# PSUM's eight banks divided among the engines that empty them, in a graph kernel's first layer

## The chip, the cores and the metric

The kernel runs on one core of one Trainium2 chip. A core has several engines with instruction streams of their own: TensorE (PE in the profile; its weight loads are PEld), VectorE (DVE), ScalarE (ACT), GpSimd (POOL) and SyncE (SP), which here issues transfers. Products and transposes of TensorE land in PSUM, which has eight banks; a bank holds 512 float32 values for each of 128 partitions. The metric is the device time of one execution in microseconds (us); lower is better.

## The reference

The input is 16 graphs of 1024 nodes with 128 features each, a dense symmetric-pattern adjacency with random positive weights (about 6% of the entries, and the diagonal), and a mask of ones. Two residual layers follow each other:

```
# layer 0
h = relu(layernorm(x))
for W, b in three layers:
    h  = h @ W + b
    nh = h / max(norm(h), 1e-12)
    ew = adj * (nh @ nh.T)            # per graph, 1024 x 1024
    h  = ew @ h                       # relu, but for the last
x = x + h
# layer 1
h = relu(layernorm(x))
keep = dilate(adj > 0)                # row by row, each row's removals change later rows
adj_d = adj * keep
three SAGE layers on adj_d with batch norm, then one linear map
x = x + that
```

The dilation depends on the adjacency alone, not on layer 0, so the kernel does it beside layer 0.

## The kernel before

**Layer 0.** The function `layer0()` is a generator. It walks over 48 stages: the graphs in pairs, each pair through the three convolutions, the two graphs of a pair taking turns. The list is `order`; of a stage `now`, `then` is the next, `after` the one behind it, and `ended` a graph that has just had its last convolution. A stage has eight steps s, one for each row q of 128-wide blocks, in the order SEQ = (0, 7, 1, 6, 2, 5, 3, 4). `ew` is as symmetric in its cosine part as `nh @ nh.T` is, so only the blocks on and above the diagonal are multiplied out. In a step:

- `products(s)`: TensorE multiplies the row's blocks of `nh @ nh.T` into PSUM tiles pg, of up to four blocks (L324). VectorE multiplies them with the adjacency, into ew in SBUF: the diagonal block at L333, the others at L336, which writes the row's blocks twice, with the weights of both triangles.
- `sums`, three steps behind (LAG): products of ew and the scaled features into po, which holds two banks (L364).
- `turn`: one step behind, the lower triangle's blocks are transposed on TensorE (gt, L353) and brought back to ew by ScalarE (L354).
- `sums_back`: products of the turned blocks into po (L378). After the last row ScalarE takes po up as hTo (L387).
- `adjT_tile` for the adjacency of a graph to come: transposes into pt_a (L240), taken up by ScalarE (L241), and stored for layer 1 by POOL (L242).
- `features` for the next stage at steps 4 and 5: products into pw (L273), taken up by VectorE as hN (L277 or L283). `turned` at step 6: transposes into pt_n, taken up by ScalarE as nhT (both L165 and L166, in `transposed`). `scaled`: squares on ScalarE (L299), the root (L157), and the scaling on POOL (L301).
- At the change from a pair to the next: `norm` and `enter` for the graphs that come (layer norm; transposes into pt_h, taken up by ScalarE); for the graphs that have ended `fetch` (the input is loaded again) at step 1, `residual` at step 3 (eight transposes into two tiles px, L398; VectorE adds the input, L401; POOL stores x2, L404) and `next_layer` at step 5 (layer norm for layer 1, stored by POOL, L410).

**The dilation.** The generator `dilation()` loads rows of the adjacency (an, L545), makes patterns on ScalarE (L547, L548), multiplies with what earlier rows kept (kl, L551; VectorE, L554), transposes small 16-bit tiles (pdt, pT; taken up by ScalarE, L571 and L580), iterates with counts in a tiny tile pc (L632, L633; VectorE), transposes pe (L681, ScalarE L682), and then runs for each row a scan of 1024 elements on VectorE (L699), an absolute value on ScalarE (L708) and a compare (L719), stored by POOL (L720).

**The order.** The main loop takes a unit of the dilation, and then as many units of layer 0 as the weights that both yield allow (COLS, TURN and SPREAD set the pace). This gives program order. The Tile framework then orders each engine's stream when the program is built, with program order as priority, and puts in the semaphores; a tile of a pool with n buffers waits until the tile n places before it under its tag is released. An engine runs its stream strictly in order. Behind layer 0 stand a branch (L768) that redoes the dilation exactly if the fast one was off (not taken for this input), the last graph's residual, and layer 1.

**PSUM.** Four pools hold the banks: ps_sm two for mt, pt_a, pt_h, pw, pt_n, px, pdt, pT, pc, pe and pf, whoever empties them; ps_g two for pg; ps_o one tile of two banks for po; ps_t two for gt. In SBUF, x2, h and h0 share two buffers under the tag tt, the loaded inputs two under xb, and the transposed features two under hT.

Of the kernel before, what the change touches and what calls it, by code (L numbers as in the profile page):

```python
# [8 lines left out]
F32 = mybir.dt.float32  # L9
F16 = mybir.dt.float16  # L10
# [3 lines left out]
PSUM = bass.MemoryType.PSUM  # L14
DRAM = bass.MemoryType.DRAM

P = 128
# [20 lines left out]
COLS, TURN = 0.215, 0.109  # L38
# [8 lines left out]
def tile_adj_preln_d2(  # L47
# [40 lines left out]
    nc = tc.nc  # L88
    B, N, D = x.shape
    NCH = N // P  # L90
    NB = B * NCH
    HALF = min(512, N)
    NHALF = N // HALF
    CPH = HALF // P
    GT = 4
# [16 lines left out]
    x2_d = [dram.tile([N, D], F32, tag=f"x2{b}", name=f"x2{b}") for b in range(B)]  # L112
# [47 lines left out]
    def transposed(psum_pool, dst, src, nm, func=AF.Copy, halves=range(NHALF)):  # L160

        for h in halves:
            pt = psum_pool.tile([P, CPH, P], F32, tag="sm", name=f"pt_{nm}_{h}")
            for c in range(CPH):
                nc.tensor.transpose(pt[:, c, :], src[:, h * CPH + c, :], ident)  # L165
            nc.scalar.activation(dst[:, h * CPH : (h + 1) * CPH, :], pt, func)  # L166


    with ExitStack() as actx:
        pool1 = actx.enter_context(tc.tile_pool(name="a1", bufs=1))  # L170
        pool2 = actx.enter_context(tc.tile_pool(name="a2", bufs=2))
        ps_sm = actx.enter_context(tc.tile_pool(name="a_sm", bufs=2, space=PSUM))
        ps_g = actx.enter_context(tc.tile_pool(name="a_g", bufs=2, space=PSUM))
        ps_o = actx.enter_context(tc.tile_pool(name="a_o", bufs=1, space=PSUM))
        ps_t = actx.enter_context(tc.tile_pool(name="a_t", bufs=2, space=PSUM))

        w0 = pool1.tile([P, 3, P], F32, name="w0")
        b0 = pool1.tile([P, 3, P], F32, name="b0")
# [23 lines left out]
        nc.scalar.dma_start(mi, nodemask.rearrange("b (c p) -> (b c) p", p=P))  # L202
        mfl = pool2.tile([P, NCH, P], F32, tag="tt", name="mfl")[:NB, 0, :]
        nc.vector.tensor_copy(mfl, mi)
        mt = ps_sm.tile([P, NB], F32, tag="sm", name="mt")
        nc.tensor.transpose(mt, mfl, ident[:NB, :NB])
        mf_flat = mf.rearrange("p b c -> p (b c)")
        nc.vector.tensor_copy(mf_flat, mt)
# [20 lines left out]
        def adjT_tile(b, q):  # L229

            place, nat, row = adj_place(b, q), Nat.pop((b, q)), NCH - q
            if row > 1:
                nc.sync.dma_start(
                    place[:, row:, :].rearrange("p c q -> p (c q)"), adj[b][q * P : (q + 1) * P, (q + 1) * P :]
                )
            for c in range(0, row, CPH):
                n = min(CPH, row - c)
                pt = ps_sm.tile([P, CPH, P], F32, tag="sm", name=f"pt_a{b}_{q}_{c}")
                for i in range(n):
                    nc.tensor.transpose(pt[:, i, :], nat[:, c + i, :], ident)  # L240
                nc.scalar.activation(place[:, c : c + n, :], pt[:, :n, :], AF.Copy)  # L241
            nc.gpsimd.dma_start(adjT_d[b][q][:, q * P :], place[:, :row, :].rearrange("p c q -> p (c q)"))  # L242

        class Batch:
# [15 lines left out]
            def enter(self, h):  # L260
                if h == 0:
                    self.hT = pool2.tile([P, NCH, P], F32, tag="hT", name=f"hT_{self.b}")
                transposed(ps_sm, self.hT, self.h, f"h{self.b}", halves=(h,))

            def features(self, h):

                nm, l, rn = f"{self.b}_{self.l}", self.l, self.rn
                if h == 0:
                    self.hN = pool1.tile([P, NCH, D], F32, tag="hN", bufs=1, name=f"hN_{nm}")
                hc = slice(h * CPH, (h + 1) * CPH)  # L270
                pw = ps_sm.tile([P, CPH, P], F32, tag="sm", name=f"pw_{nm}_{h}")
                for c in range(CPH):
                    nc.tensor.matmul(  # L273
                        pw[:, c, :], lhsT=self.hT[:, h * CPH + c, :], rhs=w0[:, l, :], start=True, stop=True
                    )
                if rn is None:
                    nc.vector.tensor_tensor(  # L277
                        self.hN[:, hc, :], pw, b0[:, l : l + 1, :].to_broadcast([P, CPH, P]), ALU.add
                    )
                else:  # L280
                    for c in range(CPH):
                        n = h * CPH + c
                        nc.vector.scalar_tensor_tensor(  # L283
                            self.hN[:, n, :], pw[:, c, :], rn[:, n : n + 1], b0[:, l, :], ALU.mult, ALU.add
                        )

            def turned(self):

                nhT = pool1.tile([P, NCH, P], F32, tag="nhT", bufs=2, name=f"nhT_{self.b}_{self.l}")
                transposed(ps_sm, nhT, self.hN, f"n{self.b}_{self.l}")  # L290
                self.next_nhT = nhT.rearrange("p c q -> p (c q)")

            def scaled(self):
# [50 lines left out]
            def turn(self, s, ew):  # L344

                q = SEQ[s]
                row = NCH - q
                for c in range(1, row, CPH):
                    n = min(CPH, row - c)
                    pt = ps_t.tile([P, CPH, P], F32, tag="gt", name=f"gt_{self.b}_{self.l}_{q}_{c}")  # L350
                    at = row + c - 1
                    for i in range(n):
                        nc.tensor.transpose(pt[:, i, :], ew[:, at + i, :], ident)  # L353
                    nc.scalar.activation(ew[:, at : at + n, :], pt[:, :n, :], AF.Copy)  # L354
# [34 lines left out]
                    )  # L389
                    self.l += 1  # L390

            def residual(self):
                b = self.b
                self.x2 = x2 = pool2.tile([P, NCH, D], F32, tag="tt", name=f"x2_{b}")
                for h in range(NHALF):
                    pt = ps_sm.tile([P, CPH, P], F32, tag="sm", name=f"px_{b}_{h}")
                    for c in range(CPH):
                        nc.tensor.transpose(pt[:, c, :], self.hT[:, h * CPH + c, :], ident)  # L398
                    for c in range(CPH):
                        n = h * CPH + c  # L400
                        nc.vector.scalar_tensor_tensor(  # L401
                            x2[:, n, :], pt[:, c, :], self.rn[:, n : n + 1], self.xb[:, n, :], ALU.mult, ALU.add
                        )
                nc.gpsimd.dma_start(x2_d[b].rearrange("(c p) d -> p c d", p=P), x2)  # L404

            def next_layer(self):
                b = self.b
# [11 lines left out]
        def layer0():  # L419
# [26 lines left out]
            for i, now in enumerate(order + [None]):  # L446
# [5 lines left out]
                for s in range(NCH if now else LAG):  # L452
                    q = SEQ[s]
# [24 lines left out]
                    if ended:  # L478
                        if s == 1:
                            ended.fetch()  # L480
                        if s == 3:
                            ended.residual()
                            yield NCH * TURN
                        if s == 5:
                            ended.next_layer()
                    if s == 5 and after and first(i + 2):
                        after.fetch()
# [39 lines left out]
        def dilate(k, half, exact):  # L527
# [14 lines left out]
            for i in range(BH):  # L542
# [21 lines left out]
                if i % GT == GT - 1:  # L564
                    four = range(i - GT + 1, i + 1)
                    bs_ = slice(i - GT + 1, i + 1)
                    pdt = ps_sm.tile([P, GT, P], F16, tag="sm", name=f"pdt{nk}_{i}")
                    for n, ii in enumerate(four):
                        nc.tensor.transpose(pdt[:, n, :], pattern(ii)[:, diag], ident16)
                    dT = pool2.tile([P, GT, P], F16, tag="dT", bufs=1, name=f"dT{nk}_{i}")  # L570
                    nc.scalar.activation(dT, pdt, AF.Copy)  # L571
                    nc.vector.tensor_scalar(rbias[:, bs_], rest[:, bs_], 2.0, -2.0, ALU.mult, ALU.add)
                    yield 0.1
                    pT = ps_sm.tile([P, GT, P], F32, tag="sm", name=f"pT{nk}_{i}")
                    for n, ii in enumerate(four):
                        nc.tensor.matmul(pT[:, n, :], lhsT=dT[:, n, :], rhs=upto, start=True, stop=False)
                        nc.tensor.matmul(pT[:, n, :], lhsT=pattern(ii)[:, diag], rhs=off, start=False, stop=False)
                        nc.tensor.matmul(pT[:, n, :], lhsT=ident16, rhs=after, start=False, stop=True)
                    for n, ii in enumerate(four):
                        nc.scalar.activation(T[:, ii, :], pT[:, n, :], AF.Identity, bias=rbias[:, ii : ii + 1])  # L580
                    yield 0.1
# [24 lines left out]
            def removals(x, nm):  # L606
# [13 lines left out]
                else:  # L620
# [4 lines left out]
                        nc.vector.tensor_tensor(ev, ev, x, ALU.is_gt)  # L625
                        nc.vector.scalar_tensor_tensor(par, x, 1.0, ev, ALU.is_gt, ALU.mult)
                    nc.vector.tensor_tensor(E, T, mid.unsqueeze(2).to_broadcast([P, BH, P]), ALU.is_equal)
                pc = ps_sm.tile([P, BH], F32, tag="sm", name=f"pc_{nm}")
                for i in range(BH):
                    c = pc[:, i : i + 1]  # L630
                    if ends:
# [44 lines left out]
            if ends:  # L676
                nc.vector.tensor_tensor(Z, Z, par.unsqueeze(2).to_broadcast([P, BH, P]), ALU.mult)
                nc.vector.tensor_tensor(E, E, Z, ALU.add)
            pe_ = ps_sm.tile([P, BH, P], F16, tag="sm", name=f"pe{nk}")
            for i in range(BH):  # L680
                nc.tensor.transpose(pe_[:, i, :], E[:, i, :], ident16)  # L681
            nc.scalar.activation(E, pe_, AF.Copy)  # L682
# [62 lines left out]
            while at * total < done * SPREAD * total0 and step0():  # L745
                pass

        pf = ps_sm.tile([1, B // 2], F32, tag="sm", name="pf")
        nc.tensor.matmul(pf, lhsT=ones_col, rhs=astray, start=True, stop=True)
        off_f = pool1.tile([1, 1], F32, name="off_f")  # L750
        nc.vector.tensor_reduce(off_f, pf, mybir.AxisListType.X, ALU.add)
# [374 lines left out]
```

## Time and profile before

| | us |
|---|---|
| runs shown (3): median | 2925.94 |
| lowest, highest | 2923.68, 2931.75 |
| the profiled execution | 2932.24 |
| its span, first to last instruction | 2930.4 |
| TensorE busy | 2673.3 (91%) |
| VectorE busy | 1955.9 (67%) |
| ScalarE busy | 1420.2 (48%) |
| GpSimd busy | 452.9 (15%) |
| granted TensorE clock, mean | 0.976 |

The last eviction of a turned block (L354) ends the first layer's main part at about 1723 us; layer 1 takes the rest. An engine's busy time is the time in which it worked on an instruction. A line of the view of waits names the engine, its tile and line, who released it, and then the microseconds in all, how often, and the longest. A line of the view of windows gives for each engine the busy time and the instructions in a stretch of the span. "L324" is line 324 of the kernel before.

### The profile page before, as it was taken

The numbers are of one execution on the slowest core, as the hardware profiler recorded it, in microseconds if no ns is written. First come the engines' busy times: TensorE is split into PE (matmuls) and PEld (weight loads), VectorE is DVE, ScalarE is ACT, GpSimd is POOL, SyncE is SP. The second block draws the span as 40 slices with busy tenths as digits, with TensorE's granted clock in tenths as the row PEclk, the third lists the DMA queues.
The fourth block names the chain that finished last, engine by engine and source line by source line (L and its number), as shares of the span: only waits on it lengthen the run. The fifth ranks groups of instructions, "written<-read, shape, count | busy, mean of one in ns | idle before, by whom it ended". The sixth has DMA issues, their size and how long they took to land.

```text
span 2930.4 us, 51972 instructions
## 1 busy us (share of the span) xinstructions
PE 2673.3 (91%) x18803; PEld 2205.6 (75%) x18803; DVE 1955.9 (67%) x4945; ACT 1420.2 (48%) x4069; POOL 452.9 (15%) x604
## 2 busy tenths in 40 slices
PE   5898998998989989998998979999989999899996
PEld 3666666666666666766666758989979999899996
DVE  2777778877977878788778446777772233455555
ACT  5766667557546546455455323333333333333333
POOL 2111112012011112121112002222220010010010
PEclk9999999999999999999999989999999999999998
DMA  8437258247347456386162039999995666576763
GB/s 268 145 115 219 89 168 247 77 139 229 92 130 219 105 169 188 95 248 176 39 206 105 1 114 403 405 406 404 405 372 173 208 210 202 177 243 222 240 217 115
DMA packets 383017, 585.21 MB, mean 200 GB/s; under 512 B 85201, under 2 KB 267345, under 8 KB 382753
## 3 DMA queue, kind: packets, MB, share of 16 engines
q1 hardware_dynamic: 343280, 425.28, 45.9%
q0 software_dynamic: 38464, 156.07, 14.4%
q8 instruction: 151, 2.47, 0.3%
q14 instruction: 114, 0.93, 0.1%
q10 hardware_dynamic: 1008, 0.46, 0.1%
HBM read 403.44 MB, written 163.58 MB: 193 GB/s over the span
## 4 chain that ended last, share of the span: by engine, by line
PE 56%; DVE 18%; DMA 13%; issue 6%; ACT 4%; POOL 1%; SPq 1%; POOLq 0%; DVEq 0%; another core or an unknown queue 0%; ACTq 0%
PE agg L831 20%; PE po L364 7%; PE pg L324 6%; DVE rank L699 5%; PE pw L803 5%; PE po L378 5%; DVE ew L336 4%; DMA aT<-in_adj_dram 3%; PE gt L353 3%; PE pp L1016 2%; DMA kl<-keep 2%; PE pw L273 2%; DMA an<-in_adj_dram 2%; DMA aT<-adjT 1%; DMA kb<-keep 1%
## 5 line engine op out<-in xcount | busy, mean ns | idle before, releaser
L831 PE MATMUL agg<-hw,aT 128*128 128x128 f32 (+1 forms) x6144 | 742.9, 277 | 8.8 <-DVE aT L941 7.5
L831 PEld LDWEIGHTS agg<-hw,aT 128*128 128x128 f32 x6144 | 712.1, 192 | 14.7 <-DVE aT L941 10.1
L324 PE MATMUL pg<-nhT 128*128 128x512 f32 (+3 forms) x1152 | 457.4, 500 | 71.9 <-DVE ew L336 63.0
L364 PE MATMUL po<-ew,hS 128*128 128x512 f32 (+3 forms) x1152 | 455.3, 499 | 13.8 <-ACT hTo L387 9.9
L336 DVE TENSOR_TENSOR ew<-pg,adjA 128x768 f32<-128x768 f32 (+3 forms) x528 | 425.1, 827 | 4.6 <-DVEq L768 2.7
L378 PE MATMUL po<-ew,hS 128*128 128x128 f32 x2688 | 366.9, 277 | 0.0
L378 PEld LDWEIGHTS po<-ew,hS 128*128 128x128 f32 x2688 | 339.3, 193 | 36.6 <-issue 36.3
L354 ACT ACTIVATE ew<-gt 128x512 f32<-128x512 f32 (+1 forms) x480 | 208.9, 465 | 243.2 <-PE gt L353 240.2
L324 PEld LDWEIGHTS pg<-nhT 128*128 128x128 f32 x1152 | 188.7, 193 | 171.6 <-issue 120.9
L699 DVE TENSOR_TENSOR_SCAN rank<-patt 128x1024 f16<-128x1024 f16 x128 | 294.0, 2307 | 0.9
L364 PEld LDWEIGHTS po<-ew,hS 128*128 128x128 f32 x1152 | 195.8, 194 | 105.6 <-issue 72.9
L353 PEld LDWEIGHTS gt<-ident,ew 128*128 128x128 f32 x1344 | 167.8, 143 | 97.3 <-issue 68.5
L333 DVE TENSOR_TENSOR ew<-pg,adjA 128x128 f32<-128x128 f32 x384 | 108.1, 282 | 196.3 <-PE pg L324 150.9
L353 PE MATMUL gt<-ident,ew 128*128 128x128 f32 x1344 | 212.1, 277 | 4.1 <-ACT ew L354 2.7
L881 POOL TENSOR_TENSOR o<-o,rn 128x512 f32<-128x512 f32 x96 | 107.6, 1121 | 650.4 <-DVE rn L880 646.0
L803 PE MATMUL pw<-wrx,hT 128*128 128x256 f32 x768 | 181.1, 391 | 10.2 <-ACT hT L1006 9.7
L805 DVE TENSOR_TENSOR own<-pw,bs 128x256 f32<-128x256 f32 x192 | 81.4, 424 | 148.0 <-ACT hw L804 148.0
L803 PEld LDWEIGHTS pw<-wrx,hT 128*128 128x128 f32 x768 | 146.3, 196 | 32.7 <-ACT hT L1006 10.5
L959 ACT ACTIVATE aT<-pta 128x512 f32<-128x512 f32 (+3 forms) x160 | 71.2, 466 | 205.0 <-PE pta L958 178.0
L860 DVE SCALAR_TENSOR_TENSOR o<-agg,invdeg,own 128x128 f32<-128x128 f32 x384 | 109.7, 344 | 87.0 <-PE agg L831 78.3
L876 ACT ACTIVATE own<-o 128x128 f32<-128x128 f32 x384 | 114.6, 301 | 103.3 <-DVE o L860 103.2
L301 POOL TENSOR_TENSOR hS<-hN,rn 128x1024 f32<-128x1024 f32 x48 | 94.6, 1970 | 409.2 <-DVE rn L157 300.4
(161 smaller groups left out, 3962.2 us busy)
## 6 DMA issues: line engine op xcount, KB each, us to landing
an<-in_adj_dram SPq DMA_DIRECT2D x128, 512.0 KB, 4.6
keep<-kp POOLq DMA_DIRECT2D x128, 256.0 KB, 3.6
kb<-keep SPq DMA_DIRECT2D x128, 256.0 KB, 5.4
aT<-adT SPq DMA_DIRECT2D x32, 960.0 KB, 5.4
aT<-adT SPq DMA_DIRECT2D x32, 832.0 KB, 5.5
aT<-adT SPq DMA_DIRECT2D x32, 704.0 KB, 4.6
aT<-adT SPq DMA_DIRECT2D x32, 576.0 KB, 3.4
xb<-in_x_dram SPq DMA_DIRECT2D x31, 512.0 KB, 5.1
```

The source lines that it names most:

```text
L324: nc.tensor.matmul(pg[:, :n, :].rearrange("p c q -> p (c q)"), lhsT=self.nhT[:, q * P : (q + 1) * P], rhs=self.nhT[:, (q + c) * P : (q + c ...
L333: nc.vector.tensor_tensor(ew[:, 0, :], pg[:, 0, :], place[:, 0, :], ALU.mult)
L336: nc.vector.tensor_tensor(both[0][:, :, off, :], pg[:, own:n, :].unsqueeze(1).to_broadcast([P, 2, n - own, P]), both[1][:, :, off, :], ALU ...
L353: nc.tensor.transpose(pt[:, i, :], ew[:, at + i, :], ident)
L354: nc.scalar.activation(ew[:, at : at + n, :], pt[:, :n, :], AF.Copy)
L364: nc.tensor.matmul(self.po[:, c * P : (c + n) * P], lhsT=self.hS[:, q, :], rhs=ew[:, c - q : c - q + n, :].rearrange("p c q -> p (c q)"), ...
L378: nc.tensor.matmul(self.po[:, q * P : (q + 1) * P], lhsT=self.hS[:, q + n, :], rhs=ew[:, NCH - 1 - q + n, :], start=False, stop=closes and ...
L699: nc.vector.tensor_tensor_scan(rank, pt[:, 1 : N + 1], pt[:, 2:], 0.0, ALU.add, ALU.add)
L803: nc.tensor.matmul(pw[:, i, :], lhsT=hT[:, 2 * h + i, :], rhs=wrx[:, l, :], start=True, stop=True)
L831: nc.tensor.matmul(self.place(c), lhsT=aT[:, blk, :], rhs=self.hw[:, source, :], start=source == 0 and c % self.ga == 0, stop=ends(c, source),
L860: nc.vector.scalar_tensor_tensor(self.o[:, c, :], self.place(c)[:, :P], invdeg[:, b, c : c + 1], self.own[:, c, :], ALU.mult, ALU.add,)
L876: nc.scalar.activation(self.own[:, n, :], self.o[:, n, :], AF.Square, accum_out=ss[:, c : c + 1])
```

## The change

The banks are divided by the engine that empties them. ps_v has one bank, for the tiles that VectorE takes up (mt, pw, px, pc, pf). ps_s has two, for those of ScalarE (pt_a, pt_h, pt_n, gt, pdt, pT, pe). ps_g has three instead of two, for pg. ps_o stays. The residual of a graph is made in two halves, the first at step 3 and the second, with the store of x2, at step 6; the layer norm behind it (`next_layer`) moves from step 5 to step 7. The weights yielded stay the same in sum. For the last graph both halves follow each other, as before.

```diff
-        ps_sm = actx.enter_context(tc.tile_pool(name="a_sm", bufs=2, space=PSUM))
-        ps_g = actx.enter_context(tc.tile_pool(name="a_g", bufs=2, space=PSUM))
+
+        ps_v = actx.enter_context(tc.tile_pool(name="a_v", bufs=1, space=PSUM))
+        ps_s = actx.enter_context(tc.tile_pool(name="a_s", bufs=2, space=PSUM))
+        ps_g = actx.enter_context(tc.tile_pool(name="a_g", bufs=3, space=PSUM))
         ps_o = actx.enter_context(tc.tile_pool(name="a_o", bufs=1, space=PSUM))
-        ps_t = actx.enter_context(tc.tile_pool(name="a_t", bufs=2, space=PSUM))
...
-                pt = ps_sm.tile([P, CPH, P], F32, tag="sm", name=f"pt_a{b}_{q}_{c}")
+                pt = ps_s.tile([P, CPH, P], F32, tag="sm", name=f"pt_a{b}_{q}_{c}")
...
-                transposed(ps_sm, self.hT, self.h, f"h{self.b}", halves=(h,))
+                transposed(ps_s, self.hT, self.h, f"h{self.b}", halves=(h,))
...
-                pw = ps_sm.tile([P, CPH, P], F32, tag="sm", name=f"pw_{nm}_{h}")
+                pw = ps_v.tile([P, CPH, P], F32, tag="sm", name=f"pw_{nm}_{h}")
...
-                transposed(ps_sm, nhT, self.hN, f"n{self.b}_{self.l}")
+                transposed(ps_s, nhT, self.hN, f"n{self.b}_{self.l}")
...
-                    pt = ps_t.tile([P, CPH, P], F32, tag="gt", name=f"gt_{self.b}_{self.l}_{q}_{c}")
+                    pt = ps_s.tile([P, CPH, P], F32, tag="sm", name=f"gt_{self.b}_{self.l}_{q}_{c}")
...
-            def residual(self):
+            def residual(self, halves=range(NHALF)):
                 b = self.b
-                self.x2 = x2 = pool2.tile([P, NCH, D], F32, tag="tt", name=f"x2_{b}")
-                for h in range(NHALF):
-                    pt = ps_sm.tile([P, CPH, P], F32, tag="sm", name=f"px_{b}_{h}")
+                if 0 in halves:
+                    self.x2 = pool2.tile([P, NCH, D], F32, tag="tt", name=f"x2_{b}")
+                x2 = self.x2
+                for h in halves:
+                    pt = ps_v.tile([P, CPH, P], F32, tag="sm", name=f"px_{b}_{h}")
...
-                nc.gpsimd.dma_start(x2_d[b].rearrange("(c p) d -> p c d", p=P), x2)
+                if 1 in halves:
+                    nc.gpsimd.dma_start(x2_d[b].rearrange("(c p) d -> p c d", p=P), x2)
...
-                        if s == 3:
-                            ended.residual()
-                            yield NCH * TURN
-                        if s == 5:
+                        if s == 3 or s == 6:
+                            ended.residual((s // 6,))
+                            yield CPH * TURN
+                        if s == 7:
                             ended.next_layer()
...
-                    pdt = ps_sm.tile([P, GT, P], F16, tag="sm", name=f"pdt{nk}_{i}")
+                    pdt = ps_s.tile([P, GT, P], F16, tag="sm", name=f"pdt{nk}_{i}")
...
-                    pT = ps_sm.tile([P, GT, P], F32, tag="sm", name=f"pT{nk}_{i}")
+                    pT = ps_s.tile([P, GT, P], F32, tag="sm", name=f"pT{nk}_{i}")
...
-                pc = ps_sm.tile([P, BH], F32, tag="sm", name=f"pc_{nm}")
+                pc = ps_v.tile([P, BH], F32, tag="sm", name=f"pc_{nm}")
...
-            pe_ = ps_sm.tile([P, BH, P], F16, tag="sm", name=f"pe{nk}")
+            pe_ = ps_s.tile([P, BH, P], F16, tag="sm", name=f"pe{nk}")
```

More of the change, by code (lines that the diff above doesn't have):

```diff
@@ L204, in tile_adj_preln_d2 @@
         nc.vector.tensor_copy(mfl, mi)
-        mt = ps_sm.tile([P, NB], F32, tag="sm", name="mt")
+        mt = ps_v.tile([P, NB], F32, tag="sm", name="mt")
         nc.tensor.transpose(mt, mfl, ident[:NB, :NB])
@@ L746, in tile_adj_preln_d2 @@
                 pass
-        pf = ps_sm.tile([1, B // 2], F32, tag="sm", name="pf")
+        pf = ps_v.tile([1, B // 2], F32, tag="sm", name="pf")
         nc.tensor.matmul(pf, lhsT=ones_col, rhs=astray, start=True, stop=True)
```

## Prediction

> **What bounds the kernel now.** I read the page's table of engines first, then a table by stage, then who TensorE, ScalarE and VectorE wait for in the stage that the change touches. Windows: the stretch, busy us of PE, PEld, DVE, ACT and POOL (instructions), granted TensorE clock, DMA share, GB/s.
>
> ```profile
> PE 2673.3 (91%) x18803; PEld 2205.6 (75%) x18803; DVE 1955.9 (67%) x4945; ACT 1420.2 (48%) x4069; POOL 452.9 (15%) x604
> ...
> 60.00:1600.00 1540.00, 1396.62 (x8734) 1016.25 (x8733) 1218.52 (x2853) 915.69 (x2430) 242.94 (x314) 0.98 0.53 154
> 1600.00:1710.00 110.00, 109.54 (x622) 79.76 (x620) 50.56 (x121) 36.81 (x114) 8.78 (x7) 1.00 0.02 6
> ...
> 870.00:880.00 10.00, 5.95 (x39) 4.59 (x38) 8.66 (x18) 5.34 (x13) 1.98 (x3) 0.98 1.13 287
> 880.00:890.00 10.00, 10.00 (x61) 7.92 (x59) 6.40 (x22) 6.02 (x19) 1.61 (x3) 0.85 1.00 330
> ```
>
> TensorE bounds the whole (91%). The first layer runs to about 1726 us. From 1600 on it is alone, and TensorE idles 0.5 us in 110: nothing is to be gained there. From 60 to 1600 us the dilation runs between its instructions, and TensorE idles 1540 − 1397 = 143 us. All that another division of PSUM can win is in those 143 us. Who it waits for there (us in total, times, longest), and the two helpers:
>
> ```profile
> PE pg L324 <- DVE ew L336: 61.9, 48, 3.6
> PE po L364 <- ACT hTo L387: 9.9, 7, 3.5
> PE pt_h L165 <- DVE x L401: 6.0, 5, 1.6
> PE pg L324 <- DVE rn L157: 6.0, 5, 1.8
> PE pt_a L240 <- DVE hN L277: 4.7, 5, 1.8
> PE pt_a L240 <- DVE hN L283: 4.2, 3, 2.3
> PE gt L353 <- ACT ew L354: 2.7, 2, 1.6
> ...
> ACT ew L354 <- PE gt L353: 183.8, 115, 5.2
> ACT patt L547 <- DMA an<-in_adj_dram: 70.4, 29, 6.8
> ACT patt L547 <- DVE rank L699: 68.4, 50, 3.8
> ...
> DVE ew L333 <- PE pg L324: 111.1, 80, 5.8
> ```
>
> The lines for pg sum to 70.1 us: a product waits for a bank that VectorE has not yet multiplied out. The transposes wait for a bank 29 us in all, and for gt only 2.7, as it has two banks to itself. ScalarE is not full (916 of 1540), but it is held in order: its next eviction may stand behind an L547 that waits up to 6.8 us for a load, or up to 3.8 for the pattern slot that a scan (2.3 us, 128 of them) frees. The timeline shows one such place; these rows give start, duration and, in brackets, the idle time before:
>
> ```profile
> 1055.38 0.52 ACT L547 ACTIVATE patt<-an 128x384 f16<-128x384 f32 x1 [2.82 <-DVE rank L699]
> ...
> 1059.07 0.38 PE L353 MATMUL gt<-ident,ew 128*128 128x128 f32 x2
> ...
> 1059.20 0.52 ACT L547 ACTIVATE patt<-an 128x384 f16<-128x384 f32 x1 [0.98 <-DVE rank L699]
> ```
>
> **The change, part by part.** It adds and removes no arithmetic. The built programs keep the places of stages and dilation against each other within some 6 us of TensorE work. What changes is how much TensorE work stands between the last instruction into a bank and the first of the next tile in it; I call that the cover. I price the work between by two chain rows, and set it against the turnaround: the trace's time from the tile's last matmul to the end of the instruction that reads it.
>
> ```profile
> 608.44 0.87 PE pt_a L240 x8
> ...
> 675.77 1.73 PE pg L324 x4
> ```
>
> A transpose is 0.11 us (0.87/8); a product of 512 columns is two instructions, so 128 columns cost 1.73/8 = 0.22. Median and ninth-decile turnarounds in the trace are 1.48 and 3.98 us for pg, 0.69 and 2.31 for gt, 0.75 and 3.34 for pt_a, 0.76 and 3.12 for pt_n.
>
> (1) *Third bank for products.* Median cover grows from 4.4 to 6.6 us; places with under 2 us fall from 58 to 3 of 574. Turnaround less cover, where positive, sums to 91.6 us before against 70.1 measured, a ratio of 0.77; after it sums to 15.7. Where VectorE idles under 15% around the place (69.7 → 14.9) a saved wait is worth (54.8 × 0.77) = 42.2 at most, and nothing if VectorE is itself the limit there: TensorE then only waits later, for ew. Elsewhere (21.6 → 0.8) I count it whole: 20.8 × 0.77 = −16.0.
>
> (2) *ScalarE's tiles share two banks.* Before, gt had two and pt_a, pt_h, pt_n, pdt, pT and pe two more, with the VectorE tiles. Now all of ScalarE's have two. Median cover: gt 5.6 → 3.1 us (under 2 us: none → 113 of 480), pt_a 3.0 → 1.8, pt_n 2.4 → 1.4. The shortfall grows from 58.7 (gt 11.4, pt_a 18.2, pt_n 13.3, pt_h 15.6) to 155.6 (gt 51.8, pt_a 55.3, pt_n 37.1). What was measured before for these is 29.2, a ratio of 0.50. Where VectorE has room it goes from 21.7 to 81.1: 59.4 × 0.5 = +29.7; where it is full, 36.8 to 74.1: +18.7. Behind a transpose that waits stand TensorE's next products and sums; VectorE waits for those, and then the dilation's chain. Bounds: 0, if ScalarE takes tiles up sooner when TensorE stalls, and 96.9, if each shortfall is paid.
>
> Where VectorE is full, (1) and (2) net −23.5. Both ends are open: 0 and −23.5. I count a third, −7.8, nearer to nothing, because DVE is busy 8.66 of the 10 us of the slice at 870 while TensorE has 5.95.
>
> (3) *VectorE's tiles in one bank, sums unchanged.* The shortfall of po goes from 21.4 to 17.7, measured 9.9, so −3.7 × 0.46 = −1.7; that of pw, px and pc from 13.4 to 16.3, at ScalarE's ratio +1.4 (bounds 0 and +2.9): −0.3. That px does not cost more is the halves' doing: back to back, its second half would wait for four L401 of 0.34 us.
>
> (4) *Residual in halves, LN two steps later.* x2 is whole at step 6, not 3; a stage has 31 us of TensorE work, 3.9 a step, so its store (POOL) leaves some 12 us later. x2 shares two buffers with the next odd batch's h, which ScalarE's LN writes behind the second half at the seven changes of pairs; the seven covers are 7, 13, 8, 8, 8, 9 and 3 us. L401's four (1.1 us together), POOL's 0.9 and 5.8 to land (median of the DMA view for L404, longest 8.4) make 7.8: short by 0.8 and 4.8 at two places, 5.6 in all, and by 19 with the longest landing everywhere. ScalarE would wait in LN, with every eviction behind it. I take half of 5.6, +3, bounds 0 and +19. The re-fetch of x on SP has three steps of slack; the LN's h0 store on POOL waits for nothing new.
>
> (5) *The end.* The branch (L768) now has only three sums_back behind it on TensorE; it takes 3.4 us on its queue, of which 0.8 and 1.1 us show as idle now: +1, bounds 0 and +3.4. Start: pt_a comes ahead of mt, nothing, since mt waits 17.6 us for the mask's load anyway.
>
> (6) *Clock.* The slice 870 to 880 has 4 us of idle TensorE, and the next is granted 0.85: 10 × 0.15 = 1.5 us. Among ScalarE's new shortfalls are 10.3, 4.6, 3.4 and 3.2 us; among the pg waits that go, the longest is 3.6. I take one more such slice, +1.5, bounds −3 and +6.
>
> [...]
>
> Sum: −16.0 + 29.7 − 7.8 − 0.3 + 3 + 1 + 1.5 = **+11.1**. The profiled run took 2932.24 us (span 2930.4; some 1.8 lie around it), so 2943.3; it lies 6.3 over the median of the runs, 2925.94, so about **2937**.
>
> **Rivals.** 0.3% (8.8 us) is about what can be told from no change.
> A, the forecast: the transposes' waits outweigh the products'.
> B, the other side: the third bank pays in full, where VectorE is full too, and ScalarE's tiles wait half as much as by their ratio. −(16.0 + 42.2) + 48.4/2 + 5.2 (steps 3 to 6) = −29: 2897. For it: 61.9 us is one line, the largest wait of all; a transpose held on TensorE gives ScalarE time to catch up. Against: 42 of the 58 lie where VectorE has next to no time left. It decides once the transposes' waits for ScalarE stay under some 73 us in all (29 of before, and 58.2 − 5.2 − 8.8 = 44 more, with the products paid in full; at half the growth it is 53).
> C, a wash: VectorE and ScalarE only exchange which is late; TensorE's idle stays 143 ± 9: 2926. For it: the dilation's chain (scans 294 us, rounds through pc) sets the pace in full stretches.
> D, waits cascade: each ScalarE shortfall is paid whole, as L547's blocked waits catch gt too: −58.2 + 96.9 + 5.2 = +44: 2970. For it: 138.8 us of L547's waits on ScalarE; against: the ratio 0.50 of before.
>
> **How the numbers follow.** A 0.35, B 0.32, C 0.18, D 0.15. Range: 2890, 7 under B, leaves out the lower quarter of B (0.08); 2968, just under D's full price, leaves out most of D (0.12). The likeliest case alone: with the full stretches at −23.5 it falls into C, at 0 it is 2945, with the longest landings of (4) and the clock's upper bound 20 more; so 2935 to 2960. A, taken as the part of it that can be told from no change, and D are slower (0.50), B faster (0.32), C the same (0.18).
>
> **What would show it.** Right: `pg <- DVE ew` falls from 62 to under 20 us, the waits of gt, pt_a and pt_n for ScalarE's evictions grow from 29 to some 75, and 60 to 1600 becomes some 8 us longer. B: the same fall of pg, with ScalarE's waits under 73 and TensorE's idle near 115. D: over 110 for the transposes, with the DVE waiting for pg or gt behind them. Step 4 shows as ScalarE's LN waiting for a DMA of x2; step 5 as idle at the branch. It is wrong if VectorE, given products earlier, orders its scans later, so that L547 and with it ScalarE shift: the cover was counted on the built order, the turnarounds on the old pace.

## The result, and the profile after

The changed kernel takes 2936.53 us (median of 20 runs, 2926.34 to 2944.52), the kernel before 2929.55 (20 runs, 2919.28 to 2935.49). The ratio is 1.0025, with a 95% interval of 1.0015 to 1.0035: some 7 us slower. The profiled execution of after took 2932.43 us, 4 under its median, with a span of 2930.4; that of before lay 3 over its own. So the two spans are equal by chance, and the traces show where time goes rather than how much.

The table of stages of after (columns as before; the rows from 60 to 1600 and from 1600 to 1710 us), then TensorE's waits from 60 to 1600 us:

```profile
60.00:1600.00 1540.00, 1389.09 (x8727) 1007.18 (x8726) 1207.37 (x2847) 915.57 (x2428) 248.35 (x314) 0.99 0.52 154
1600.00:1710.00 110.00, 109.53 (x620) 79.67 (x619) 50.57 (x120) 36.90 (x114) 8.66 (x6) 1.00 0.02 6
```

```profile
PE gt L354 <- DVE ew L337: 31.4, 46, 4.1
PE pt_a L241 <- ACT ew L355: 16.3, 10, 2.7
PE pt_n L165 <- ACT ew L355: 14.9, 10, 2.2
...
PE gt L354 <- ACT ew L355: 9.4, 11, 1.7
PE pt_h L165 <- ACT adjA L242: 8.9, 3, 4.4
...
PE pg L325 <- DVE ew L337: 5.2, 4, 2.6
```

The wait that led the list, pg for VectorE's L336, has gone from 61.9 to 5.2 us. Two kinds have come in its place: transposes that wait for ScalarE to empty one of its two banks (pt_a, pt_n, gt, pt_h), and gt, which waits for ew: not for a bank, but for the very blocks that VectorE has yet to multiply. TensorE's idle time from 60 to 1600 us went from 143 to 151 us. That the span didn't grow is the clock's doing in this one execution (it withheld 20.5 us in this stage, and 29.0 in before); the last section comes back to it. Over all executions the clock differs the other way: the kernel before was granted 0.979 of full speed in the mean (63 executions beside the experiments), the changed one 0.976 (20). A clock lower by 0.003 withholds some 9 us in 2930, about as much as the kernels differ in time.

To compare kernels I add up that view's lines by what is waited for. "Transposes, ScalarE" are gt, pt_a, pt_n, pt_h, pdt, pT and pe where an instruction of ScalarE let them go; pdt waiting for patt and pT for dT, which is data and not a bank, are left out. The next column has pt_a, pt_n and pt_h let go by VectorE, and "gt for ew" is gt let go by VectorE. Waits for loads, and those of pw, px and pe for VectorE, are not in the table. In the light pair (e5, e6) the last scan ends near 1505 and 1550 us, before at 1594; its sums are of the same window.

| us in 60 to 1600 | pg | transposes, ScalarE | pt_a, pt_n, pt_h, VectorE | gt for ew | pc | po | ratio to before |
|---|---|---|---|---|---|---|---|
| before | 70.1 | 9.9 | 19.3 | 1.3 | 12.3 | 10.4 | 1 |
| after | 6.2 | 73.1 | 1.0 | 33.4 | 11.5 | 8.1 | 1.0025 |
| e1, banks alone | 1.8 | 65.5 | 1.5 | 35.9 | 13.7 | 5.5 | 1.0023 |
| e2, halves alone | 72.3 | 11.0 | 24.1 | 0.0 | 11.3 | 7.3 | 1.0081 |
| e3, six shared | 5.1 | 14.3 | 5.3 | 50.8 | 32.2 | 25.9 | 1.0111 |
| e4, three and three | 30.5 | 26.6 | 2.5 | 50.2 | 15.2 | 14.3 | 1.0062 |
| e5, light scan, before | 11.6 | 11.9 | 3.6 | 0.0 | 12.5 | 14.8 | 0.9762 |
| e6, light scan, after | 2.7 | 60.9 | 0.2 | 9.7 | 11.5 | 8.9 | 0.9821 |
| e7, turn two behind, after | 14.4 | 53.3 | 0.8 | 0.0 | 24.3 | 31.4 | 1.0087 |
| e8, turn two behind, before | 84.3 | 13.6 | 17.8 | 0.0 | 14.2 | 4.2 | 1.0061 |
| e9, pace 0.91, before | 73.1 | 4.6 | 20.4 | 1.9 | 8.8 | 8.1 | 0.9989 |
| e10, pace 0.91, after | 2.0 | 55.3 | 0.0 | 39.9 | 6.4 | 4.5 | 0.9992 |
| e11, ScalarE has three | 64.3 | 24.1 | 1.7 | 0.5 | 10.9 | 6.1 | 0.9961 |
| e12, one more slot, before | 71.6 | 8.2 | 18.0 | 1.3 | 12.4 | 6.1 | 1.0018 |

The intervals of the ratios are about ±0.0015, and ±0.002 for e2 to e8.

### The profile page after: what moved, and what is told of

Read it like the earlier page. It is cut to its first block, busy times and chain, and to the rows that moved or that the text cites. A ratio compares the mean times of both kernels' runs of the same rounds, so it can differ in the third digit from the quotient of the medians.

```text
span 2930.4 us, 52053 instructions
## 1 busy us (share of the span) xinstructions
PE 2667.4 (91%) x18803; PEld 2197.0 (75%) x18803; DVE 1947.2 (66%) x4945; ACT 1421.9 (49%) x4069; POOL 459.2 (16%) x604
## 3 DMA queue, kind: packets, MB, share of 16 engines
q0 software_dynamic: 38464, 156.07, 14.2%
## 5 line engine op out<-in xcount | busy, mean ns | idle before, releaser
L835 PEld LDWEIGHTS agg<-hw,aT 128*128 128x128 f32 x6144 | 711.2, 192 | 14.2 <-DVE aT L945 9.7
L365 PE MATMUL po<-ew,hS 128*128 128x512 f32 (+3 forms) x1152 | 443.6, 491 | 9.4 <-ACT hTo L388 8.1
L354 PEld LDWEIGHTS gt<-ident,ew 128*128 128x128 f32 x1344 | 161.3, 142 | 181.3 <-issue 77.0
L354 PE MATMUL gt<-ident,ew 128*128 128x128 f32 x1344 | 222.9, 280 | 63.4 <-DVE ew L337 31.4
L334 DVE TENSOR_TENSOR ew<-pg,adjA 128x128 f32<-128x128 f32 x384 | 107.5, 280 | 205.7 <-PE pg L325 151.8
```

The costliest lines, as they stand in the source:

```text
L365: nc.tensor.matmul(self.po[:, c * P : (c + n) * P], lhsT=self.hS[:, q, :], rhs=ew[:, c - q : c - q + n, :].rearrange("p c q -> p (c q)"), ...
L835: nc.tensor.matmul(self.place(c), lhsT=aT[:, blk, :], rhs=self.hw[:, source, :], start=source == 0 and c % self.ga == 0, stop=ends(c, source),
```

## The experiments

**Which part does it: the banks or the halves?** e1 takes the halves back.

```diff
-                        if s == 3 or s == 6:
-                            ended.residual((s // 6,))
-                            yield CPH * TURN
-                        if s == 7:
+                        if s == 3:
+                            ended.residual()
+                            yield NCH * TURN
+                        if s == 5:
                             ended.next_layer()
```

> The changed kernel's banks (one, two, three, two), with the residual whole at step 3 and next_layer at step 5 as before. Theory 1 (the banks decide; ScalarE's two banks take back what the third bank for products gives): 4 to 12 us slower than before, like the changed kernel; TensorE's waits of pg for VectorE near 6 us, those of the transposes for ScalarE near 75. Theory 2 (the banks gain and the halves lose: x2's store holds ScalarE's layer norm, and the second half stands before the transposes of step 6): as fast as before or up to 8 us faster, with no wait of the layer norm for a transfer of x2. Theory 3 (any new order of the instructions moves the time by this much, whatever its banks): anything within 10 us either way, and waits that do not follow the banks.

The ratio is 1.0023 (1.0008 to 1.0038), 2933.68 us in the median: what the changed kernel has, with the same exchange of waits. The banks alone make the result; theory 2 falls, and theory 3 too, as the waits follow the banks. Where the time goes its profiled execution doesn't show: TensorE idles 138 us from 60 to 1600 us, 5 fewer than before, the first layer ends 6 us earlier (1717 us), and 8 us are lost behind it, for a reason that no run shows. e2 is the other half, the edit of `residual` and of steps 3, 6 and 7 in the kernel before.

> The banks of before, with the residual in halves at steps 3 and 6 and next_layer at step 7. Theory 1: within 5 us of before; pg's waits stay near 70 us, the transposes' near 30. Theory 2: 5 to 20 us slower than before, with ScalarE's layer norm waiting for a transfer of x2 (some 5 us at a place) and longer waits of pt_n. Theory 3: anything within 10 us.

It is 0.81% slower (1.0062 to 1.0101), against theories 1 and 3. Its waits in the table are those of before (loads of the adjacency hold pt_a up 7 us longer, 13.0 for 5.9), and ScalarE's layer norm waits for no transfer there, against the reason that theory 2 gave. The profiled execution is 2939.74 us, the fastest of its six runs (median 2950.69), so it shows little of the loss. What it shows is the end: the layer norm that moved to step 7 and the branch now stand in front of the last gt on TensorE (waits from 1700 to 1740 us):

```profile
PE gt L353 <- PEq L771: 2.5, 1, 2.5
PE gt L353 <- DVE ln_mv_l L141: 2.2, 1, 2.2
PE px L400 <- ACT hTo L387: 1.1, 1, 1.1
```

Before, TensorE waited there 0.8 us for the branch. These 4 us are a part of the 23; the rest isn't settled. With the new banks the halves cost nothing that e1 and the changed kernel can tell apart (0.0002 ± 0.002).

**Is it the number of banks that a tile can take?** The prediction's count (shortfall: turnaround less cover) says that six banks shared by all should all but end the waits for banks.

```diff
-        ps_sm = actx.enter_context(tc.tile_pool(name="a_sm", bufs=2, space=PSUM))
-        ps_g = actx.enter_context(tc.tile_pool(name="a_g", bufs=2, space=PSUM))
+        ps_sm = actx.enter_context(tc.tile_pool(name="a_sm", bufs=6, space=PSUM))
...
-        ps_t = actx.enter_context(tc.tile_pool(name="a_t", bufs=2, space=PSUM))
...
-                    pg = ps_g.tile([P, CPH, P], F32, tag="pg", name=f"pg_{nm}_{c}")
+                    pg = ps_sm.tile([P, CPH, P], F32, tag="sm", name=f"pg_{nm}_{c}")
...
-                    pt = ps_t.tile([P, CPH, P], F32, tag="gt", name=f"gt_{self.b}_{self.l}_{q}_{c}")
+                    pt = ps_sm.tile([P, CPH, P], F32, tag="sm", name=f"gt_{self.b}_{self.l}_{q}_{c}")
```

> All six banks that hold no sums in one pool, whoever empties them; residual whole. Counted on its built order as in the prediction, the shortfall is 18 us for pg (91.6 before) and 38 for ScalarE's tiles (59 before). Theory 1 (it is banks per tile that matter, and a shared pool gives each tile the longest cover): 20 to 45 us faster than before, at the weights that came out for the change (0.41 for pg, 0.5 for ScalarE's): -30 - 10 = -40. Rival (VectorE sets the pace in the full stretches, so that a product that comes sooner only makes the transposes wait for ew): within 10 us of before, with TensorE's idle time between 60 and 1600 us at 130 to 150 and the wait of gt for VectorE's ew above 30.

It is 1.11% slower (1.0092 to 1.0130): theory 1 misses by some 70 us, and the rival names the wait but not its size. The waits for banks did end (pg 5.1 us, transposes 20), as counted. In their place TensorE waits for data, as the first lines of its waits show:

```profile
PE gt L351 <- DVE ew L334: 49.3, 64, 2.5
PE pc L631 <- DVE E L625: 23.2, 20, 3.4
PE po L362 <- ACT hTo L385: 18.0, 14, 4.1
```

In the built program of e3, pc's matmuls stand on average 2.5 us of TensorE work earlier against the first layer's than before; in the changed kernel it is 0.3. TensorE asks sooner for what VectorE's rounds of the dilation have yet to make, and pc's waits go from 12 to 32 us. That this order is the cause is argued from the place and the wait, not tried apart. It can't be all: of the 31 us by which e3's profiled execution is longer, 20 lie in the first layer and 11 behind it. e4 gives three banks to all that VectorE empties (pg, pw, px and pc share ps_g) and three to ScalarE, residual whole.

> The division by engine kept, but three banks for all that VectorE empties (pg, pw, px, pc share them) and three for ScalarE; residual whole. Shortfall on the built order: pg 66, ScalarE's 56. Theory 1: 3 to 20 us faster than before (-25 x 0.41 - 2.5 x 0.5 = -11), with the transposes' waits for ScalarE back at 30 us. Rival (the division by engine is itself what costs): as slow as the changed kernel, some 7 us over before.

0.62% slower (1.0042 to 1.0082), again with fewer waits for banks (60 us for 99), and gt for ew at 50 us; both theories miss. Its pc stands 1.8 us earlier in the trace's order, and yet waits only 3 us longer than before. So a count of bank waits alone, on which the prediction rests, does not give the time of another division: what a freed product does next has to be counted too.

**Is the third bank's gain lost because VectorE is full?** e5 and e6 shorten the dilation's scan in both kernels; TensorE's order in e5 is that of before.

```diff
-                    ranks[i] = rank = pool2.tile([P, N], F16, tag="rank", bufs=3, name=f"rank{nk}_{i}")
-                    nc.vector.tensor_tensor_scan(rank, pt[:, 1 : N + 1], pt[:, 2:], 0.0, ALU.add, ALU.add)
+                    ranks[i] = rank = pool2.tile([P, N // 4], F16, tag="rank", bufs=3, name=f"rank{nk}_{i}")
+                    nc.vector.tensor_tensor_scan(
+                        rank, pt[:, 1 : N // 4 + 1], pt[:, 2 : N // 4 + 2], 0.0, ALU.add, ALU.add
+                    )
```

> The kernel before, with the dilation's scan over 256 of 1024 columns (ScalarE's absolute value reads that quarter four times, so it is as long as before), and the exact branch never taken: the dilation's result is left out of what is computed rightly. VectorE has some 128 x 1.7 = 218 us less to do between 60 and 1600 us; TensorE's order is that of before. All theories: 40 to 120 us faster than before, as TensorE's idle time for pg falls from 70 to 10-30 us. It is the mate of the next kernel.

> The same lighter scan in the changed kernel. Theory 1 (the third bank's gain is lost where VectorE is full: what TensorE no longer waits for a bank, it waits for ew): here gt's wait for VectorE's ew is under 10 us (31 in the changed kernel), and the kernel is as fast as its mate or up to 15 us faster. Rival (VectorE's load has no part in it; ScalarE's two banks alone cost): it is 5 to 15 us slower than its mate, as the changed kernel is than the kernel before, with the transposes' waits for ScalarE near 75 us.

e5 takes 2853.27 us (0.9762, 0.9743 to 0.9782), e6 2877.22 (0.9821, 0.9804 to 0.9838): with a light scan the change costs 0.6%, 17 us by the ratios and 24 by the medians, more than the 0.25% under full load. The first lines of the waits of e5, then of e6:

```profile
PE po L364 <- ACT hTo L387: 14.3, 12, 2.6
PE pg L324 <- DVE ew L336: 11.6, 19, 1.5
```

```profile
PE gt L354 <- ACT ew L355: 17.2, 12, 4.3
PE pt_h L165 <- ACT adjA L242: 13.2, 3, 6.3
PE pc L637 <- DVE E L631: 10.2, 12, 1.9
PE gt L354 <- DVE ew L337: 9.7, 10, 3.8
```

Theory 1 foresaw gt's wait for ew rightly (9.7) and the time wrongly, and so had the thing the wrong way round. The rival has the direction, with a cost that is larger than its 5 to 15 us. With a lighter VectorE, pg waits 11.6 us in place of 70 and a third bank has next to nothing to win. ScalarE's shortage is there at either load: its transposes wait 46 us more than in the mate (61.1 against 15.5), nearly as under full load (45). But these waits are not the price. Others fell meanwhile, and TensorE's idle time grew by 17 us, as the rows of e5 and e6 from 60 to 1500 us show; the granted clock fell too (third from the end):

```profile
60.00:1500.00 1440.00, 1357.41 (x8665) 997.00 (x8663) 1008.90 (x2828) 901.49 (x2414) 240.69 (x312) 0.99 0.55 164
60.00:1500.00 1440.00, 1340.39 (x8421) 984.91 (x8421) 976.75 (x2738) 874.36 (x2337) 228.64 (x296) 0.97 0.54 160
```

In this stretch the clock withheld 10 us in e5 and 38 in e6. The two profiled executions are the fastest of four and the slowest of four, and lie 43 us apart. Over the four of each the granted clock is 0.982 and 0.975 in the mean, some 20 us of time for a difference of 24. So in this pair the clock takes most of the time; in the traces of before and after it falls after idle times of some 2 us (last section).

**Can the wait for ew be turned into time?** e7 and e8 turn each row two steps behind its products.

```diff
-                    if s > 0 and now or s == 0 and i:
-                        b_, *of = behind[-2 if now else -1]
-                        if now or s == 0:
-                            b_.turn(*of)
-                            yield (NCH - 1 - SEQ[of[0]]) * TURN
+                    if s > 1 and now or i and s < 2:
+                        b_, *of = behind[-3 if now else 0]
+                        b_.turn(*of)
+                        yield (NCH - 1 - SEQ[of[0]]) * TURN
```

> The changed kernel, with each row's turn (gt) two steps behind its products in place of one, so that TensorE asks for ew later. Theory 1a (the wait of gt for ew is TensorE's own, and giving it time removes it): gt's wait for VectorE falls from 31 us to under 10, and the kernel is 10 to 30 us faster than the changed kernel, thus faster than before. Theory 1b (VectorE and the dilation's chain set the pace in these stretches; the wait only moves on to the next one in TensorE's order): the waits of gt fall, those of pc, po or pg grow by as much, and the time stays within 8 us of the changed kernel or gets worse, as VectorE's stream now has the dilation some 6 us of first-layer work further back.

> The same in the kernel before. Theory 1a: no gain, -5 to +5 us, since gt waits for ew only 1.3 us there and pg waits for banks. Theory 1b: 0 to 15 us slower, as the dilation stands 6 us further back on VectorE with nothing to win on TensorE.

gt no longer waits for ew in e7 (33 to 0), and the kernel is 0.87% slower than before (1.0071 to 1.0102): po's waits rise from 8 to 31 us, pc's from 12 to 24, pg's from 6 to 14. Theory 1b holds: the wait moves on to the next thing in TensorE's order that needs VectorE. TensorE's idle time is that of the changed kernel (153 and 151 us), and of the some 15 us that e7 takes longer the clock accounts for a part (0.974 and 0.976 over the runs, some 7 us). e8 is 0.61% slower (1.0045 to 1.0077), some 15 to 18 us: at the upper end of 1b or just over it, and against 1a.

**Is it only another order?** e9 and e10 lay the dilation earlier against the first layer, in both kernels.

```diff
-SPREAD = 0.93
+SPREAD = 0.91
```

> The kernel before with SPREAD 0.91 in place of 0.93: the same work and banks, the dilation laid some 13 us earlier against the first layer, so that nearly every bank wait meets another neighbour. Theory B (banks): its distance to the kernel before is the pace's, and its distance to the next kernel is the banks'. Theory O (any new order costs, since the order of before happens to be a good one): 5 to 30 us slower than before. If the pace has room: up to 10 us faster, as the dilation's end comes earlier.

> The changed kernel with SPREAD 0.91. Theory B: 3 to 12 us slower than its mate with the banks of before, with the same exchange of waits (pg for VectorE from 60-80 us to under 10; the transposes for ScalarE from 30 to 60-90; gt for ew from under 5 to 30). Theory O: the difference to its mate is anything from -15 to +15 us, though the waits are exchanged in the same way.

e9 is at 0.9989 (0.9973 to 1.0005), e10 at 0.9992 (0.9978 to 1.0007). The waits change places just as at the other pace: pg 73 to 2 us, the transposes 25 to 55, gt for ew 2 to 40. The times are equal within some 6 us, where theory B had e10 3 to 12 us slower. Theory O had e9 5 to 30 us slower than before, which it isn't; the difference between the two it left open, and there it is not excluded. So the exchange of waits belongs to the banks. Its net does not: 7 us at one pace, 1 at the other. The granted clock goes with the times: 0.976 and 0.977 over the runs here, equal as they are, and 0.979 and 0.976 for the pair at the other pace.

**Where should the sixth bank go?** e11 is the changed kernel with that bank moved from the products to ScalarE.

```diff
-        ps_s = actx.enter_context(tc.tile_pool(name="a_s", bufs=2, space=PSUM))
-        ps_g = actx.enter_context(tc.tile_pool(name="a_g", bufs=3, space=PSUM))
+        ps_s = actx.enter_context(tc.tile_pool(name="a_s", bufs=3, space=PSUM))
+        ps_g = actx.enter_context(tc.tile_pool(name="a_g", bufs=2, space=PSUM))
```

> The changed kernel with the sixth bank given to ScalarE (three) in place of the products (two). Theory B: pg's waits are back at 60-75 us, the transposes' waits for ScalarE at 15-35, gt's for ew under 10; the time is that of before within 8 us: it loses the third product bank's gain and ScalarE's cost at once. Rival (what costs is the halves, which cost 23 us with the banks of before): 15 to 25 us slower than before.

It is the fastest kernel here that does the whole work: 2917.06 us, 0.9961 of before (0.9949 to 0.9973), and 0.64% or some 19 us below the changed kernel, from which it differs in this bank alone. TensorE's waits and its row of the stage:

```profile
PE pg L325 <- DVE ew L337: 58.6, 52, 3.2
PE pc L637 <- DVE E L631: 9.5, 14, 1.2
PE pt_a L241 <- ACT ew L355: 7.9, 8, 3.3
```

```profile
60.00:1600.00 1540.00, 1408.42 (x8828) 1030.92 (x8826) 1217.69 (x2869) 921.51 (x2449) 253.98 (x317) 0.98 0.52 154
```

Against after, the products wait for banks again (64 us for 6), and the transposes' waits for ScalarE have fallen from 73 to 24 us and gt's for ew from 33 to 0.5. TensorE idles 132 us, 12 fewer than before and 19 fewer than after, about the differences in time. Against before, pt_a, pt_n and pt_h no longer wait behind a VectorE tile in a shared bank (19.3 to 1.7 us), but the transposes wait 14 us longer for ScalarE; the rest of the 12 us is spread over small lines. So this division is a gain of some 11 us, more than the 8 that theory B allowed; the rival (the halves) falls for these banks. That dividing by the engine is the reason is not shown: e4 divides so as well, with pw, px and pc among the products' banks, and is 0.62% slower than before.

**Are ScalarE's evictions held up by the pattern slots?** e12 adds one.

```diff
-        SLOTS = BH + 2
+        SLOTS = BH + 3
```

> The kernel before with one pattern slot more (BH + 3), so that ScalarE's L547 waits less for a scan to free one; TensorE's order is unchanged. If ScalarE's blocked evictions are what makes its banks scarce: ScalarE's wait of L547 for the scan falls from 68 us to under 45, the transposes' waits fall by some 5 us, and the kernel is 3 to 12 us faster than before. If not: the wait falls, and the time stays within 5 us.

It is at 1.0018 (1.0003 to 1.0033), and ScalarE's L547 waits 79.9 us for the scan in place of 68.4. The slot didn't take away the wait that it was to take away, so the question stays open. There is another candidate that no run tries apart. ScalarE's eviction of pe stands in its stream before pe is ready; in before and in after it waits

```profile
ACT E L682 <- PE pe L681: 10.4, 8, 3.8
ACT E L686 <- PE pe L685: 50.5, 9, 13.3
```

with all later evictions behind it. It doesn't decide alone, since it waits 47.6 us in e11 too, the fastest.

## Why the prediction was right

It gave 2937 us, and 2936.53 were measured, with the direction and the exchange of waits of case A. That the time agrees to a microsecond is luck: the prediction started from a median of 2925.94 us, which 20 runs put at 2929.55, and added 11.1 us where 7.0 were measured. By its own measure of 0.3%, and by C's idle time of 143 ± 9 us (151 measured), the size lies in C; the 20 runs resolve it as slower. By its steps:

- *Step 1.* pg under 20 us: 6.2. The saved 64 us were priced at 30 (16 where VectorE has room, and a third of 42). Half came back: gt waits 32 us more for ew, the wait that the step named ("TensorE then only waits later, for ew"). Net 32.
- *Step 2.* The transposes from 29 to some 75 us: 74.1. Their price in time is not shown: in the light pair the same growth of these waits (46 us) went with 17 us of idle time and a lower clock. The prediction's reason for what makes ScalarE late (L547's blocked waits) stayed untested.
- *The third that was counted in full stretches* was a choice between two ends and came out near. Its reason was too simple: the light pair shows that the third bank has something to win only where VectorE is loaded (pg's waits 70 us, 11.6 with a light scan), and under that load half of it came back as gt's wait; where there is room there is next to nothing to win, against the 16 us that step 1 counted there.
- *Step 3.* pw, px and pc fell by some 6 us in all, and po by 2.3 us, for 1.7 foreseen.
- *Step 4.* The wait is there, once and of the size worked out for one place (4.8), and e1 shows that it does not set the time. The +3 was not to be had:

```profile
ACT h L148 <- DMA x<-x: 4.7, 1, 4.7
```

- *Step 5.* At the end TensorE waits 1.3 us for the branch (0.8 before), 1.3 for px's one bank, and no longer 1.1 for pg. Its +1 is not seen; the last stage ends no later than before.
- *Step 6.* Mis-sized. The profiled pair shows the reverse (11 dips of the clock in this stage, 14 before), but over the runs after is withheld some 9 us more than before, beyond the step's upper bound of 6. In executions of one and the same kernel, a us more withheld goes with about half a us more time (0.54, fitted over all runs). So an estimate of the clock's share is between 5 us and all of the 7, and 2 us or nothing are left for the waits themselves.

By that estimate the exchange of waits, priced at 5.6 us, is near a wash, and the clock, priced at 1.5, carries most of the difference; what in the new order of waits lowers it was not tried apart. The +3 and +1 did not show. The sum came near since these miss each other. Had the count been trusted alone, it would have failed: it gave e3 as 40 us faster. What probably kept it near here is that the change all but leaves pc's place on TensorE alone, and that half of the products' gain was set aside for the wait that comes next.

## What to carry to other kernels

Dividing PSUM banks by the engine that empties them can pay, but how decides: with one bank for VectorE's small tiles, three for ScalarE's and two for the products it won 0.39%, with two and three it lost 0.25%. Here the sixth bank was worth more at ScalarE (2917.06 us), which is held up in its own order, than at the longest wait in the list (2936.53). The longest wait here was TensorE waiting for VectorE (61.9 us), and a bank only let it run ahead to the next thing that VectorE owed (gt waited 33.4 us for ew, 1.3 before). Before pricing a wait as gain, look for the next instruction on the waiting engine that needs the same releaser. Where a few tenths of a per cent decide, make the change at a second pace too, and compare the granted clock over all runs before dividing a difference by one pair of traces.

## What the runs showed of the hardware

From 60 to 1600 us in before and in after, TensorE's clock halves for 3.41 us, or for 6.83, after quite short idle times. In after, one wait of gt for ew of 4.1 us, which ends at 864.5, goes with this (columns as above, the granted clock is third from the end):

```profile
861.00:864.00 3.00, 0.00 (x0) 0.00 (x0) 3.00 (x3) 0.59 (x2) 0.79 (x2) 0.74 0.51 161
864.00:867.00 3.00, 2.45 (x7) 1.69 (x8) 2.95 (x7) 0.00 (x0) 0.00 (x0) 0.50 0.15 45
867.00:870.00 3.00, 3.00 (x13) 2.03 (x12) 1.57 (x3) 1.09 (x2) 0.00 (x0) 0.62 0.83 267
```

And in before, a single wait of 2.04 us for pg, which ends at 205.7, is enough:

```profile
204.00:206.00 2.00, 0.28 (x1) 0.30 (x2) 2.00 (x4) 1.37 (x2) 0.00 (x0) 1.00 0.59 185
206.00:208.00 2.00, 2.00 (x7) 1.06 (x6) 2.00 (x8) 1.97 (x6) 0.00 (x0) 0.78 0.41 119
208.00:210.00 2.00, 2.00 (x11) 2.00 (x10) 0.92 (x8) 1.72 (x5) 0.00 (x0) 0.50 0.53 141
```

The last two rows lose 2 × 0.22 + 2 × 0.50 = 1.4 us. In slices of 2 us I count 14 such dips from 60 to 1600 us in before and 11 in after, 15 in e11 and 19 in e10. The clock's own records of that stage in these two traces are 3.41 us long or a whole multiple of it, so that each stretch of 3.41 us at half clock withholds 1.71 us. They show what counts. In both together, each of the 20 stretches at full clock in which TensorE idled 2.0 us or more is followed by one at half clock; with 1.7 to 2.0 us of idle time 5 of 17 are, and with under 1.7 us none of 836. So in these traces idle time of 2 us that falls within one stretch withholds 1.7 us more behind it; short waits that are spread out do not.

All that the clock withholds in that stage adds up to 29.0 us in before and 20.5 in after. These 8.5 us make up for the 7.5 us of idle time that after has more, and that is why the two profiled spans are equal. The mean clocks of all runs lie the other way (0.979 and 0.976), so this pair does not show how the 7 us between the medians divide.
